# A state-space scan beside three convolution layers: a third PSUM bank for the scan's decays, made two ahead, and sums over states taken later

## The chip, the cores and the metric

The kernel runs on one core of one Trainium2 chip. The metric is the device time of one execution in microseconds (us). The median of three runs is 22843.68 us (22834.28 to 22850.13). A core has five engines that concern us, each with an instruction queue of its own: PE (TensorE, matrix multiplication), DVE (VectorE), ACT (ScalarE), POOL (GpSimd), and SP (SyncE), which here only issues DMAs. They meet through semaphores.

## What is computed

Four images of 128 channels and 128 x 128 pixels go through four layers. Each layer normalises its input by groups of channels and adds its result to it.

```python
x = x + _L0_conv_ref(_gn(x), ...)   # deformable 3x3 convolution (gathers rows by index)
x = x + _L1_conv_ref(_gn(x), ...)   # dilated 5x7 convolution and two 1x1
x = x + _L2_conv_ref(_gn(x), ...)   # state-space scan in four directions
x = x + _L3_conv_ref(_gn(x), ...)   # 3x3 convolution and a difference term
```

The core of layer 2, for each of four directions over the 16384 pixels, each channel and each of 16 states:

```python
dA = jnp.exp(d[..., None] * A)
h = h * dA + (d * u)[..., None] * b[:, :, None, :]
y = jnp.einsum('bkcn,bkn->bkc', h, c)
```

`dA` is what the kernel calls a decay. All data are fp32.

## The kernel before

The image is cut into 32 blocks of 4 rows, so a tile is 128 partitions x 512 pixels (2 KB per partition, one PSUM bank). The kernel uses all eight PSUM banks: two for `pa` (the decays), one for `dub`, one for `yacc`, and four "side banks", `bank(0)` to `bank(3)`, that the other layers share.

**The scan** (`scan`, from L761) is the long work. It runs over `seq`, 4 directions x 32 blocks, 128 blocks `t` for an image. The 128 channels x 16 states of a block are packed as four groups `g` of 32 channels; in each group a partition holds one channel and one of four sets of states, and four scans `ng` follow each other. One scan is a *slot*: 16 slots for each block, 2048 for each image, 8192 in all. In a group:

- DVE multiplies inputs and b for all four slots into `h` (L923, 128 x 2048); the inputs come from PSUM tile `dub`, which ACT fills (`inputs_up`, L838) in the slot `ng == 2` of the group before.
- For each slot ACT makes a decay (`decay`, L852, an exponential into `pa`), and DVE runs the scan (L963), which reads `pa` and replaces `h` in place. The decay of the next slot is issued just before the scan of this one. A `pa` tile can be written again when the scan two slots earlier has read it.
- After two scans ACT copies the last column into `carry` (`carry_on`, L887), and then POOL multiplies the two halves of `h` by c (`outputs`, L893): the first half at `ng == 2` of the same group, the second at the start of the next group. Beside layer 0 DVE takes the second half, at `ng == 2`. Where PE is the busier neighbour POOL also adds the two parts of each second half in every other group (L895), so that PE has one matmul less.
- PE sums over the states by a gathering matrix into `yacc` (`sums`, L866), and in the two backward directions adds the y of the forward pass (L871). Before the change group g's first half is summed at `ng == 2` of the next group and its second half at `ng == 3`.
- At the second group of block t (`g == 1`, `ng == 1`) `finish` has ACT copy the `yacc` of block t-1 out (L876) and stores it; `yacc` is one bank, so the next block's first sum waits for that copy.
- `prepare` (L791 to L823) makes steps, b and c of the block two ahead, in pieces, one after each slot.

**The other layers** run beside the scan: beside the scan of image b come layers 2 (after the scan) and 3 of image b-1, and layers 0, 1 and 2 (before the scan) of image b+1. They are generators; `together` lets the scan issue a slot and then pulls side work until it has reached the same share of its own length. `chain` and the weights in `head` and `tail` give these shares. Inside a layer, `weave` works through a hand-written order of groups: an entry `(n, step)` does step for the block n rounds back. `keep_order` then fixes the program order on every engine as issued. So each engine runs its queue in exactly the order in which the Python code emitted it, side work and scan mixed.

`loads` (L1221) sets `beside["busy"]` while a layer is the neighbour: "POOL" for layer 0, "PE" for layer 1, layer 2 before the scan, and the tail layers for the first images. This is how the scan knows what runs beside it.

The side banks in layer 2: before the scan, `pd2` (L637) and `pz` (L722) use bank 2 and `pv2` (L648) bank 3; after it `pd3` uses bank 0, `pv3` (L1045) bank 1, `pj3` bank 2 and `pv4` (L1071) bank 3. In both parts ACT reads a `pv` by Ln and Exp (`rsqrt`, L203 and L204), and `square` reads `pd2` twice (L643, L645). Layer 0 uses all four side banks; its table, layer 1 and layer 3 use banks 0 to 2 or fewer.

```python
for ng in range(NG):
    ...
    nc.vector.tensor_tensor_scan(o, f, o, carry[:, n : n + 1], ALU.mult, ALU.add)
    if ng == 3 and then[0] < len(seq):
        decay(*then, 0)
    next(more, None)
    yield (t * NST + n + 1) / slots
```

Of the kernel before, what the change touches and what calls it, by code (L numbers as in the profile page):

```python
# [10 lines left out]
F32 = mybir.dt.float32  # L11
# [7 lines left out]
P = 128  # L19
# [4 lines left out]
N = R * W  # L24
NBLK = H // R
KK = 9
NST = 16
# [4 lines left out]
NG = 4  # L32
# [78 lines left out]
def conv_preact_kernel(ctx: ExitStack, tc: tile.TileContext, a: dict, nb: int):  # L111
# [9 lines left out]
    pss = ctx.enter_context(tc.tile_pool(name="scps", bufs=1, space=PSUM))  # L121
# [7 lines left out]
    def bank(which, name):  # L129
        return psb.tile([P, N], F32, name=name, tag=f"bank{which}")  # L130

    waiting = []
    beside = {}

    def store(dst, src, after=3, of=None):

        waiting.append([after, of, dst, src])
# [459 lines left out]
    def layer2_pre(st):  # L597
# [6 lines left out]
        with ExitStack() as s:  # L604
# [26 lines left out]
            got = {}  # L631
# [13 lines left out]
                nc.scalar.activation(sq, pd, AF.Square, bias=shc)  # L645

            def spread_variance(i):
                got["v", i] = pv = bank(3, "pv2")  # L648
                nc.tensor.matmul(pv, jmat, got["s", i], start=True, stop=True)

            def invert(i):
# [109 lines left out]
    def scan(st, pull):  # L761
        us = st["u"]
        st["y"] = ys = (image("yrow"), image("ycol"))
        seq = []
# [3 lines left out]
            seq += [(k, i, back, back) for i in order]  # L768
        carries = {}
        blocks = [{} for _ in seq] + [None]  # L770

        def fetch(t):
            if t < len(seq):
                k, i, _, _ = seq[t]
                while st["out"] < (i + 1 if k == 0 else NBLK + 1):
                    pull()
                    tick()
                if not stored(us[0]):
                    flush()
                blocks[t]["u"] = load(sp, blk(us[k % 2], i), [P, N], "u", bufs=2)  # L780
# [64 lines left out]
                p.rearrange("p n t -> p (n t)"), src.unsqueeze(0).to_broadcast([Q, P // Q, NG * N])  # L845
            )

        def decay(t, g, ng):
            k = seq[t][0]
            n = g * NG + ng  # L850
            pa = pss.tile([P, N], F32, name="pa", bufs=2)
            nc.scalar.activation(pa, blocks[t]["p", g][:, 0, :], AF.Exp, scale=neg_a[:, k, n : n + 1])  # L852
            blocks[t]["a", n] = pa

        def sums(t, g, half):

            c = blocks[t]
            k, i, back, second = seq[t]
            if g == 0 and half == 0:
                c["y"] = pss.tile([P, N], F32, name="yacc")  # L860
            last = g == NG - 1 and half == 1
            parts = (2 * half, 2 * half + 1)
            if half and c.get(("added", g)):
                parts = parts[:1]
            for ng in parts:
                nc.tensor.matmul(  # L866
                    c["y"], gather[:, g, :], c["h", g][:, ng, :],
                    start=g == 0 and ng == 0, stop=last and ng == parts[-1] and not second,
                )
            if last and second:  # L870
                nc.tensor.matmul(c["y"], ident, c["before"], start=False, stop=True)  # L871

        def finish(t):
            k, i, back, second = seq[t]
            y = sp.tile([P, N], F32, name="y")
            nc.scalar.copy(y, blocks[t]["y"])  # L876
            store(blk(ys[k % 2], i), y, of=ys)
            blocks[t] = None
            st["summed"] = t + 1 - 3 * NBLK
# [9 lines left out]
        def outputs(t, g, half, engine=nc.gpsimd):  # L889

            c = blocks[t]
            h = c["h", g][:, 2 * half : 2 * half + 2, :]
            engine.tensor_mul(h, h, c["cb"][:, 2 * half : 2 * half + 2, :])  # L893
            if half and g % 2 and beside.get("busy") == "PE":
                engine.tensor_add(h[:, 0, :], h[:, 0, :], h[:, 1, :])  # L895
                c["added", g] = True
# [10 lines left out]
        for g in range(2):  # L907
            spread_steps(0, g)
        inputs_up(0, 0)
        decay(0, 0, 0)  # L910
        slots = len(seq) * NST
        for t, (k, i, back, second) in enumerate(seq):
            c = blocks[t]
            carry = carries[k]
            more = prepare(t + 2) if t + 2 < len(seq) else iter(())
            if t > 0:
                fetch(t + 3)
            for g in range(NG):
                then = (t, g + 1) if g + 1 < NG else (t + 1, 0)
                soon = (t, g + 2) if g + 2 < NG else (t + 1, g + 2 - NG)  # L920
                before = (t, g - 1) if g else (t - 1, NG - 1)
                c["h", g] = h = hp.tile([P, NG, N], F32, name="h")
                nc.vector.tensor_tensor(  # L923
                    h, c["pdu", g].unsqueeze(1).to_broadcast([P, NG, N]), c["bb"], ALU.mult
                )
                on_vector = beside.get("busy") == "POOL"
                if before[0] >= 0:
                    carry_on(*before, 1)
                    if not on_vector:
                        outputs(*before, 1)  # L930
                if soon[0] < len(seq):
                    spread_steps(*soon)
                decay(t, g, 1)
                if g == 1:
                    if t + 1 < len(seq):
                        spread_states(t + 1, "bb")
                if g == 2 and t + 1 < len(seq):
                    spread_states(t + 1, "cb")
                if g == 3 and second:
                    c["before"] = load(sp, blk(ys[k % 2], i), [P, N], "before")  # L940
                for ng in range(NG):
                    n = g * NG + ng
                    if ng == 1:
                        decay(t, g, 2)
                        if g == 1 and t > 0:
                            finish(t - 1)
                    if ng == 2 and before[0] >= 0 and on_vector:
                        outputs(*before, 1, nc.vector)
                    if ng == 2:
                        carry_on(t, g, 0)  # L950
                        outputs(t, g, 0)
                        decay(t, g, 3)
                        if then[0] < len(seq):
                            inputs_up(*then)
                        if before[0] >= 0:
                            sums(*before, 0)
                    if ng == 3:
                        if before[0] >= 0:
                            sums(*before, 1)
                    o, f = h[:, ng, :], c["a", n]  # L960
                    if back:
                        o, f = o[:, ::-1], f[:, ::-1]
                    nc.vector.tensor_tensor_scan(o, f, o, carry[:, n : n + 1], ALU.mult, ALU.add)  # L963
                    if ng == 3 and then[0] < len(seq):
                        decay(*then, 0)
                    next(more, None)
                    yield (t * NST + n + 1) / slots
            for _ in more:
                pass
        t = len(seq) - 1  # L970
        carry_on(t, NG - 1, 1)
        outputs(t, NG - 1, 1)
        sums(t, 3, 0)
        sums(t, 3, 1)
        finish(t)
# [3 lines left out]
    def layer2_post(st):  # L979
# [4 lines left out]
        with ExitStack() as s:  # L984
# [18 lines left out]
            got = {}  # L1003
# [64 lines left out]
                nc.scalar.activation(sq, p, AF.Square)  # L1068

            def spread_out(i):  # L1070
                got["w", i] = pv = bank(3, "pv4")  # L1071
                nc.tensor.matmul(pv, jmat, got["t", i], start=True, stop=True)

            def invert_out(i):
# [21 lines left out]
            def r(what):  # L1096
                return lambda n: what(NBLK - 1 - n)

            def ready(n):
                return st["summed"] > min(n, NBLK - 1) and stored(st["y"])  # L1100

            order = [[(0, r(fetch)), (1, r(fetch_gate)), (5, r(fetch_skip))], [(2, r(centre))],
                     [(3, r(spread_variance))], [(7, r(affine))], [(5, r(spread_out))], [(2, r(square))],
                     [(3, r(invert))], [(7, r(add))], [(5, r(invert_out))], [(4, r(project))],
                     [(3, r(gated))], [(6, r(scale))], [(7, r(measure))], [], [(4, r(square_out))], []]
            yield from weave(NBLK, order, ready)
            flush()
        st["x3"], st["stats3"] = keep, stats_out
# [109 lines left out]
    sts = [{"b": b} for b in range(nb)]  # L1218
    last = nb - 1

    def loads(engine, stage):  # L1221
        for f in stage:
            beside["busy"] = engine
            yield f
        beside.clear()

    def head(b):
        st = sts[b]
        return [(layer0_table(st), 12), (loads("POOL", layer0(st)), 28), (loads("PE", layer1(st)), 14),
                (loads("PE", layer2_pre(st)), 36)]  # L1230

    def tail(b):
        load = "PE" if b + 1 < last else None
        return [(loads(load, layer2_post(sts[b])), 16), (loads(load, layer3(sts[b])), 22)]

    first = head(0)
    drain(chain(first[:3]))
# [1 line left out]
    for b in range(nb):  # L1239
        side = [(begun, 18)] if b == 0 else tail(b - 1)  # L1240
        if b < last:
            side += head(b + 1)
        else:
            side = [(stage, 2.5 * w) for stage, w in side] + [(layer2_post(sts[b]), 33)]
        together(lambda pull: scan(sts[b], pull), chain(side))
    drain(layer3(sts[last]))
    keep_order(tc, started)
# [83 lines left out]
```

## Time and profile before

| what | us |
|---|---|
| median of 3 runs | 22843.68 |
| the profiled execution, its own time | 22841.14 |
| its span (first to last instruction) | 22839.3 |
| the first scan starts at | 2120.1 |
| the last scan starts at | 22509.2 |
| beside layer 0, in three stretches | 6100 |
| DVE scans, 8192 x 1270 ns | 10076.9 |
| DVE products into h, 2048 x 2268 ns | 4645.6 |
| ACT decays, 8192 x 686 ns | 5618.4 |
| POOL products with c, 3740 x 2360 ns | 8783.5 |
| PE sums, 15354 instructions | 8369.2 |

The busy tenths by slice, 40 slices of 571 us, show the stages: the scan begins at the end of the fourth, and the three stretches where DVE is at 9 and ACT at 8 are those beside layer 0.

```profile
PE   4558866667788887666788888666688878777778
DVE  3553889999988799889997789889998788999883
ACT  5885768887677666788768666688867866666563
POOL 4772777777887887787787798778878778877773
PEclk7669988888899998888899999888899989899899
```

In a row of the groups, the figures after the bar are the busy time, the mean length of one instruction in ns, and then the time that the engine stood idle just before these instructions, with the releaser that ended most of it. In the waits, each row names the waiting engine and line, what it waited for, the total, how often, and the longest. In a table by stretch the columns are the stretch, its length, then busy time and number of instructions of PE, PE's weight loads (PEld), DVE, ACT and POOL, the granted PE clock, the DMA share and GB/s. A line of the timeline has start, length, engine, line and operation, and in brackets the idle time before it and its releaser.

### The profile page before, as it was taken

Reading aid. Unit: us, or ns where it says so; the run is one execution under the profiler, and the core shown is the slowest. Engines: PE = TensorE matmul, PEld = TensorE weight load, DVE = VectorE, ACT = ScalarE, POOL = GpSimd, SP = SyncE. Lnnn points to the kernel's source line nnn. Section 1 sums busy time; section 2 is a strip of 40 time slices with the busy share of each in tenths; the row PEclk is TensorE's granted clock in tenths of the full one; section 3 lists DMA queues with packets and bytes.
Section 4 is the critical chain, followed back from the end, with each engine's and each line's share of the span. In section 5 each row is a group of like instructions: output and inputs, shape, how many; then the busy total and the mean of one; then the engine's idle time right before and its main releaser. Section 6 shows DMA issues by size and latency. Waiting matters only on the chain. (4 is left out here: it accounts for less than half of the span.)

```text
span 22839.3 us, 178643 instructions
## 1 busy us (share of the span) xinstructions
PE 17184.5 (75%) x38114; PEld 6655.5 (29%) x38114; DVE 18850.6 (83%) x19637; ACT 16473.3 (72%) x37410; POOL 17338.8 (76%) x11579
## 2 busy tenths in 40 slices
PE   4558866667788887666788888666688878777778
PEld 1222222223232333222333233222232323233323
DVE  3553889999988799889997789889998788999883
ACT  5885768887677666788768666688867866666563
POOL 4772777777887887787787798778878778877773
PEclk7669988888899998888899999888899989899899
DMA  8775587777665957777766775877775677555664
GB/s 241 231 219 156 193 285 241 241 240 242 217 203 188 231 199 265 241 243 244 245 215 201 200 219 205 281 241 243 245 245 196 201 203 216 185 192 200 195 200 120
DMA packets 2557775, 5005.30 MB, mean 219 GB/s; under 512 B 1056832, under 2 KB 1328648, under 8 KB 2414352
## 3 DMA queue, kind: packets, MB, share of 16 engines
q1 hardware_dynamic: 2188048, 3785.60, 50.7%
q0 software_dynamic: 368640, 1208.25, 17.9%
q8 instruction: 310, 5.08, 0.1%
q14 instruction: 777, 6.37, 0.1%
HBM read 4065.12 MB, written 857.74 MB: 216 GB/s over the span
## 5 line engine op out<-in xcount | busy, mean ns | idle before, releaser
L963 DVE TENSOR_TENSOR_SCAN h<-pa,carry,h 128x512 f32<-128x512 f32 x8192 | 10076.9, 1270 | 1516.3 <-ACT pa L852 1307.6
L893 POOL TENSOR_TENSOR h<-h,cb 128x1024 f32<-128x1024 f32 x3740 | 8783.5, 2360 | 2996.6 <-ACT carry L887 2925.3
L866 PE MATMUL yacc<-h,gather_sb 128*128 128x512 f32 x15354 | 8369.2, 678 | 1722.1 <-POOL h L893 851.3
L852 ACT ACTIVATE pa<-spread,neg_a 128x512 f32<-128x512 f32 x8192 | 5618.4, 686 | 3412.6 <-DVE h L963 3385.3
L416 POOL DMA_INDIRECT g<-table,idx x4608 | 4552.8, 988 | 1603.3 <-issue 1075.9
L923 DVE TENSOR_TENSOR h<-dub,bb 128x2048 f32<-128x2048 f32 x2048 | 4645.6, 2268 | 434.2 <-ACT dub L838 427.8
L866 PEld LDWEIGHTS yacc<-h,gather_sb 128*128 128x128 f32 x15354 | 3135.0, 216 | 6166.8 <-issue 3593.4
L430 ACT ACTIVATE g<-g,wt 128x128 f32<-128x128 f32 x9216 | 2895.2, 390 | 398.5 <-DMA g<-table,idx 394.3
L453 PE MATMUL pst<-ident,v 128*128 128x128 f32 x4608 | 1178.7, 364 | 2141.3 <-DVE v L445 1885.1
L442 DVE TENSOR_TENSOR pw<-pw,g 128x512 f32<-128x512 f32 x2304 | 1599.0, 694 | 956.9 <-ACT pw L430 900.0
L430 ACT ACTIVATE pw<-g,wt 128x128 f32<-128x128 f32 x4608 | 1693.1, 367 | 262.1 <-DVE v L445 149.3
L453 PEld LDWEIGHTS pst<-ident,v 128*128 128x128 f32 x4608 | 716.3, 158 | 3535.7 <-issue 1890.8
L463 PE MATMUL acc<-smp,w_sb 128*128 128x512 f32 x2304 | 1573.8, 773 | 15.2 <-DVE x L470 12.5
L445 DVE SCALAR_TENSOR_TENSOR v<-g,wt,pw 128x128 f32<-128x128 f32 x4608 | 1293.7, 343 | 113.4 <-DVE pw L442 2.3
L838 ACT COPY dub<-spread 128x512 f32<-128x512 f32 x2048 | 1169.1, 571 | 138.3 <-DMA spread<-stepsd 138.0
L887 ACT COPY carry<-h 128x2 f32<-128x2 f32 x4096 | 766.7, 187 | 694.2 <-DVE h L963 692.6
L807 PE MATMUL pxbc<-u,xbc_sb 128*128 128x512 f32 x1024 | 664.2, 735 | 737.9 <-DVE h L923 725.3
L791 PE MATMUL pdt<-u,wd 128*128 128x512 f32 x1024 | 626.8, 697 | 684.1 <-DVE h L923 609.6
L1164 PE MATMUL p<-xn,w_l_sb 128*128 128x508 f32 (+2 forms) x2304 | 1105.0, 599 | 1.8 <-ACT xn L1143 1.8
L703 PE MATMUL px<-win,convw_sb 128*128 128x508 f32 (+1 forms) x1536 | 851.9, 637 | 6.7 <-DMA win<-win 6.7
L705 PE MATMUL py<-win,diag 128*64 128x508 f32 (+1 forms) x1536 | 833.7, 625 | 0.0
L817 POOL TENSOR_TENSOR e<-e,one_e 128x512 f32<-128x512 f32 x512 | 668.5, 1306 | 87.1 <-ACT one_e L811 87.1
(170 smaller groups left out, 17301.6 us busy)
## 6 DMA issues: line engine op xcount, KB each, us to landing
spread<-stepsd SPq DMA_DIRECT2D x2048, 512.0 KB, 4.2
bb<-bcd SPq DMA_DIRECT2D x512, 1024.0 KB, 7.5
cb<-bcd SPq DMA_DIRECT2D x512, 1024.0 KB, 7.7
stepsd<-steps SPq DMA_DIRECT2D x512, 512.0 KB, 3.0
table<-gt SPq DMA_DIRECT2D x512, 256.0 KB, 5.9
g<-table,idx POOLq DMA_INDIRECT x4608, 3.8
u<-urow SPq DMA_DIRECT2D x256, 256.0 KB, 4.5
yrow<-y SPq DMA_DIRECT2D x256, 256.0 KB, 3.1
```

The source lines that it names most:

```text
L416: nc.gpsimd.indirect_dma_start(out=g[:, r].rearrange("p q c -> p (q c)"), out_offset=None, in_=table, in_offset=bass.IndirectOffsetOnAxis( ...
L430: nc.scalar.activation(pw[:, r * P : (r + 1) * P] if c == 0 else g[:, r, c, :], g[:, r, c, :], AF.Copy, scale=wv[:, r, q, k, c : c + 1],)
L442: nc.vector.tensor_add(pw, pw, g[:, :, c, :])
L445: nc.vector.scalar_tensor_tensor(v[:, r, :], g[:, r, 3, :], wv[:, r, q, k, 3:4], pw[:, r, :], ALU.mult, ALU.add)
L453: nc.tensor.transpose(pst[:, r * P : (r + 1) * P], v[:, r, :], ident)
L463: nc.tensor.matmul(got["a", i], w0[:, k, :], got.pop(("c", n)), start=k == 0, stop=k == KK - 1)
L838: nc.scalar.copy(p, blocks[t]["p", g][:, 1, :])
L852: nc.scalar.activation(pa, blocks[t]["p", g][:, 0, :], AF.Exp, scale=neg_a[:, k, n : n + 1])
L866: nc.tensor.matmul(c["y"], gather[:, g, :], c["h", g][:, ng, :], start=g == 0 and ng == 0, stop=last and ng == parts[-1] and not second,)
L893: engine.tensor_mul(h, h, c["cb"][:, 2 * half : 2 * half + 2, :])
L923: nc.vector.tensor_tensor(h, c["pdu", g].unsqueeze(1).to_broadcast([P, NG, N]), c["bb"], ALU.mult)
L963: nc.vector.tensor_tensor_scan(o, f, o, carry[:, n : n + 1], ALU.mult, ALU.add)
```

## The change

Four things change.

1. `loads` takes a flag `spare`, true for every neighbour but layer 0. With it, `decays` issues decays up to two slots ahead of the scan instead of one, and every third decay goes to side bank 3 as `pa3`.
2. To free bank 3, `pv2` moves to bank 2 and `pv4` to bank 1, and the hand-written order after the scan is changed around them.
3. `sums`: a group's first half is issued at `ng == 3` of the next group, its second half at `ng == 1` of the group after that.
4. `finish` is issued at `ng == 2` instead of `ng == 1`.

```diff
             def spread_variance(i):
-                got["v", i] = pv = bank(3, "pv2")
+                got["v", i] = pv = bank(2, "pv2")
...
+        ahead = {"turn": -1, "made": 0}
+        def decays(at):
+            while ahead["made"] < min(at + (2 if beside.get("spare") else 1) + 1, len(seq) * NST):
+                decay(ahead["made"])
+                ahead["made"] += 1
...
-        def decay(t, g, ng):
+        def decay(n):
+            t, n = divmod(n, NST)
+            g, ng = divmod(n, NG)
             k = seq[t][0]
-            n = g * NG + ng
-            pa = pss.tile([P, N], F32, name="pa", bufs=2)
+            turn = (ahead["turn"] + 1) % 3
+            if turn == 2 and not beside.get("spare"):
+                turn = 0
+            ahead["turn"] = turn
+            pa = bank(3, "pa3") if turn == 2 else pss.tile([P, N], F32, name="pa", bufs=2)
             nc.scalar.activation(pa, blocks[t]["p", g][:, 0, :], AF.Exp, scale=neg_a[:, k, n : n + 1])
...
+                earlier = (t, g - 2) if g > 1 else (t - 1, g + NG - 2)
...
-                decay(t, g, 1)
+                at = t * NST + g * NG
+                decays(at)
...
                     if ng == 1:
-                        decay(t, g, 2)
-                        if g == 1 and t > 0:
-                            finish(t - 1)
+                        decays(at + 1)
+                        if earlier[0] >= 0:
+                            sums(*earlier, 1)
+                    if ng == 2 and g == 1 and t > 0:
+                        finish(t - 1)
...
                         carry_on(t, g, 0)
                         outputs(t, g, 0)
-                        decay(t, g, 3)
+                        decays(at + 2)
                         if then[0] < len(seq):
                             inputs_up(*then)
-                        if before[0] >= 0:
-                            sums(*before, 0)
-                    if ng == 3:
-                        if before[0] >= 0:
-                            sums(*before, 1)
+                    if ng == 3 and before[0] >= 0:
+                        sums(*before, 0)
...
-                    if ng == 3 and then[0] < len(seq):
-                        decay(*then, 0)
+                    if ng == 3:
+                        decays(at + 3)
...
             def spread_out(i):
-                got["w", i] = pv = bank(3, "pv4")
+                got["w", i] = pv = bank(1, "pv4")
...
-                     [(3, r(spread_variance))], [(7, r(affine))], [(5, r(spread_out))], [(2, r(square))],
-                     [(3, r(invert))], [(7, r(add))], [(5, r(invert_out))], [(4, r(project))],
-                     [(3, r(gated))], [(6, r(scale))], [(7, r(measure))], [], [(4, r(square_out))], []]
+                     [(3, r(spread_variance))], [(7, r(affine))], [(2, r(square))], [(3, r(invert))], [],
+                     [(5, r(spread_out))], [(7, r(add))], [(4, r(project))], [(5, r(invert_out))],
+                     [(3, r(gated))], [(6, r(scale))], [(7, r(measure))], [(4, r(square_out))], []]
...
-    def loads(engine, stage):
+    def loads(engine, stage, spare=False):
         for f in stage:
-            beside["busy"] = engine
+            beside["busy"], beside["spare"] = engine, spare
             yield f
         beside.clear()
```

In `head`, `tail` and the last image, the layers other than layer 0 are wrapped in `loads(..., True)`.

More of the change, by code (lines that the diff above doesn't have):

```diff
@@ L909, in scan @@
         inputs_up(0, 0)
-        decay(0, 0, 0)
+        decays(-1)
         slots = len(seq) * NST
@@ L972, in scan @@
         outputs(t, NG - 1, 1)
+        sums(t, 2, 1)
         sums(t, 3, 0)
@@ L1228, in head @@
         st = sts[b]
-        return [(layer0_table(st), 12), (loads("POOL", layer0(st)), 28), (loads("PE", layer1(st)), 14),
-                (loads("PE", layer2_pre(st)), 36)]
+        return [(loads(None, layer0_table(st), True), 12), (loads("POOL", layer0(st)), 28), (loads("PE", layer1(st), True), 14),
+                (loads("PE", layer2_pre(st), True), 36)]
     def tail(b):
         load = "PE" if b + 1 < last else None
-        return [(loads(load, layer2_post(sts[b])), 16), (loads(load, layer3(sts[b])), 22)]
+        return [(loads(load, layer2_post(sts[b]), True), 16), (loads(load, layer3(sts[b]), True), 22)]
     first = head(0)
@@ L1243, in conv_preact_kernel @@
         else:
-            side = [(stage, 2.5 * w) for stage, w in side] + [(layer2_post(sts[b]), 33)]
+            side = [(stage, 2.5 * w) for stage, w in side] + [(loads(None, layer2_post(sts[b]), True), 33)]
         together(lambda pull: scan(sts[b], pull), chain(side))
```

## The prediction

> **What bounds the kernel now.** I read four views in this order: the busy times of the page, its groups by line, the waits, and the busy times by stretch; then the timeline at one stall.
>
> ```profile
> PE 17184.5 (75%) x38114; PEld 6655.5 (29%) x38114; DVE 18850.6 (83%) x19637; ACT 16473.3 (72%) x37410; POOL 17338.8 (76%) x11579
> L963 DVE TENSOR_TENSOR_SCAN h<-pa,carry,h 128x512 f32<-128x512 f32 x8192 | 10076.9, 1270 | 1516.3 <-ACT pa L852 1307.6
> L852 ACT ACTIVATE pa<-spread,neg_a 128x512 f32<-128x512 f32 x8192 | 5618.4, 686 | 3412.6 <-DVE h L963 3385.3
> L876 ACT COPY y<-yacc 128x512 f32<-128x512 f32 x512 | 295.8, 578 | 30.8 <-PE yacc L871 30.8
> ```
>
> No engine is full, VectorE is nearest, and the two middle rows are the matter: VectorE waits 1307.6 us for decays in 1076 stalls, while ScalarE waits 3385.3 us for scans before making decays. Each starves the other. The waits view says where else engines stand:
>
> ```profile
> DVE h L963 <- ACT pa L852: 1307.6, 1076, 7.4
> PEld yacc L866 <- POOL h L893: 1619.8, 1006, 7.4
> PE yacc L866 <- POOL h L893: 851.3, 521, 6.6
> PE yacc L866 <- ACT y L876: 398.0, 270, 6.5
> DVE pw L442 <- ACT pw L430: 900.0, 524, 10.7
> ```
>
> By stretch (PE, PEld, DVE, ACT, POOL) the limits differ. In order: layer 0, layer 2 before the scan, layer 2 after it, and layer 3, each beside a scan.
>
> ```profile
> 9190.00:11180.00 1990.00, 1286.15 (x3309) 525.08 (x3302) 1790.33 (x2718) 1717.84 (x4756) 1566.72 (x1375) 0.82 0.75 241
> 17200.00:18380.00 1180.00, 1031.30 (x2102) 354.58 (x2102) 951.20 (x673) 916.97 (x1684) 916.25 (x502) 0.95 0.59 195
> 7400.00:8010.00 610.00, 497.89 (x982) 186.27 (x981) 435.75 (x325) 420.95 (x817) 525.96 (x322) 0.92 0.88 222
> 19750.00:21360.00 1610.00, 1257.02 (x2714) 510.18 (x2714) 1537.53 (x1114) 975.21 (x1971) 1271.37 (x646) 0.95 0.54 195
> ```
>
> Beside layer 3 VectorE is 96% busy, in the second line it is 81% with PE at 87%, and in the third POOL leads with 86%. One stall of the second kind, ScalarE and then VectorE:
>
> ```profile
> 17499.75 1.28 ACT L735 ACT_TABLE_LOAD   x1
> 17501.04 1.06 ACT L735 ACTIVATE u<-u 128x1024 f32<-128x1024 f32 x1
> 17502.00 1.04 ACT L736 ACTIVATE z<-z 128x1024 f32<-128x1024 f32 x1
> 17503.06 1.28 ACT L737 ACT_TABLE_LOAD   x1
> 17504.35 0.69 ACT L852 ACTIVATE pa<-spread,neg_a 128x512 f32<-128x512 f32 x1
> ...
> 17505.08 1.28 DVE L963 TENSOR_TENSOR_SCAN h<-pa,carry,h 128x512 f32<-128x512 f32 x1 [4.23 <-ACT pa L852]
> 17509.07 1.28 DVE L963 TENSOR_TENSOR_SCAN h<-pa,carry,h 128x512 f32<-128x512 f32 x1 [2.71 <-ACT pa L852]
> ```
>
> A burst of side work stands between two decays in ScalarE's queue. VectorE had one decay in store, used it, and stood 4.23 us, then 2.71 us in the same burst.
>
> **What the Trainium skill says.** "Perfetto Trace Analysis", Optimization Strategy: the same gap repeating on the engine that should be saturated can mean that PSUM or SBUF ran out for the next tile. The trace fits: 1076 such gaps, with two buffers for pa. The same page, Tensor Engine Instruction, says that ScalarE, VectorE and GpSimd take instructions strictly in order; in the lines above the decay of 17504.35 does follow the side work. "PSUM — Partial Sum Buffer", Specifications: eight banks of 512 fp32 values. A 128x512 tile fills one, and the kernel uses all eight, so the third pa can only come from a side bank; no run here shows the count itself. "Perfetto Trace Analysis", Identifying the Most-Contended Engine, warns that matmul busy time misstates PE's distance from its limit. So I don't read PE's 87% as a hard ceiling; PEld is 30% in the same stretch.
>
> **The change part by part.** *Third bank, decays two ahead (outside layer 0).* No instruction is added: 8192 decays of 686 ns before and after. Decay n+2 is issued where decay n+1 was, and its bank was last read by scan n-1, the same scan that decay n+1 waited for. So ScalarE's wait for VectorE is no longer than before, and nothing queued behind it is later because of it. What changes is VectorE's store: two decays at the start of a burst. dub (571 ns), the other thing VectorE needs from ScalarE, is already issued two slots ahead.
>
> To price it I went through the timeline by stage. I took the stalls between two points at which ScalarE waited over 0.1 us for a scan (there it has caught up) as one group, and let each group give back at most one scan, 1.27 us. Stalls and what they can return: layer 2 before the scan (four stretches) 717 us, return 277; layer 2 after it (four) 348, return 162; layer 3 (three) 98, return 94; layer 0's table (three) 54, return 52; layer 1 (three) 56, return 53. Sum of returns 638. The rest, 35 us, lies in layer 0 and the tail, where no third bank is used or little is left. A store that covers a group's first operation too (four scans and one 2.27 us product per four slots, 1.84 us per slot) would return about 780.
>
> How much arrives? In layer 3, the table and layer 1 VectorE is 87% to 96% busy and the stalls are short; I take 0.9 of 199, 179 us. In the two parts of layer 2 other engines are close: taking 74 us out of 1180 raises PE from 87% to 93%, and 26 out of 610 raises POOL from 86% to 90%. I take 0.65 of 439, 285 us, a choice between a third and all.
>
> *Sums two slots (second half) and one slot (first half) later.* The same matmuls. Each now follows its POOL product by five slots, instead of four (first half) or three (second), so most of PE's 851 us wait on POOL goes. I book nothing for it: ScalarE hardly waits for PE, so PE was not holding the loop. It gives PE the room that the line above assumes. The h tile is held two slots longer; with four buffers the next write of the same one is still seven slots behind the last read (nine before), so no wait.
>
> *finish one slot later.* Its copy (578 ns) now follows the last sums by one slot, not two. In the trace those sums ended a median of 2.4 to 4.6 us before the copy beside all but layer 0, where it was 7.5; a slot is about 2.1 us there and 4.4 in layer 0. So some of the 512 copies will wait. Behind it on ScalarE stand carry, the decay and dub. Bounds: nothing, if PE runs as far ahead as its lost POOL waits allow, and 512 x 1 us if not; I take 25 us. The y store goes to SP a slot later; its nearest reader, the load of before at the turn of direction, still comes some three slots after it.
>
> *Side banks.* pv2 joins pd2 and pz in bank 2; pv4 joins pv3 in bank 1 and the order after the scan changes. The matmul of pv2 must now wait until square has read pd2 (3 groups of the weave earlier), and pv4 until Ln has read pv3 (2 groups earlier). About 256 such hand-overs, 128 of each. ScalarE reaches its next read 3 groups later; a group is about 0.6 slot in the first weave (576 slots for 38 rounds of 25 groups) and 0.4 or more in the second (256 for 39 rounds of 16), so 2.6 us or more cover a 1.0 us matmul. I cost it at nothing; uncovered, it is in the rival below. Layer 0 (6100 us of the scan) keeps its two banks and its order of decays: no gain, no loss.
>
> Sum: 179 + 285 - 25 = 439. From the profiled execution, 22841.1 us (span 22839.3 and 1.8 around it), this gives 22402; the median 22843.7 is 2.5 above that execution. Forecast 22400.
>
> **The rivals.** (1) *Only the VectorE-bound stages gain.* For it: PE at 87% to 89% before the scan, POOL at 86% after it. Against: all VectorE idle time of the second stretch is this wait (196 of 229 us). Then 179 - 25 = 154 come, 22690. (2) *The wait moves and nothing is gained:* ScalarE's bursts are as long as before, and VectorE stands later instead. For it: in the example one scan covers 1.27 of 6.94 us. Against: ScalarE still waits 162 us for scans in that stretch, so it does catch up and refills. 22840. (3) *Slower: the merged banks put PE and ScalarE on one chain.* In layer 2, PE waits for square's two reads (0.68 us each) and then ScalarE for pv2 (1.0), 2.4 us a block; after the scan Ln (0.69) and pv4 (1.0), 1.7 us. If all reach VectorE: 128 x 2.4 + 128 x 1.7 = 525 us lost against 439 gained, 22930. It decides from 439 / 256 = 1.7 us per hand-over on. For it: PE waits 398 us for y, so it does run level with ScalarE. Against: the three groups between the steps, and a stage in which PE's POOL waits end. (4) *The third bank is not used where I think:* the compiled order of the changed kernel shows every third decay in its own tile before and after the scan, so I give this nothing.
>
> **How the numbers follow.** Forecast 0.63, its own range 22150 to 22640; rival 1 0.13; rival 2 0.07; rival 3 0.17. From 22050 (the 780 us bound gives 22060) to 22850 the range leaves out rival 3 and little else. A difference under 0.2% (46 us) can't be told from none. Faster 0.76, same 0.07, slower 0.17.
>
> **What would show it.** Right: the row of the scan waits under 800 us for pa in place of 1307.6; the stretch beside layer 3 near 98% VectorE; PE's waits for h from POOL cut by half or more; y's wait for yacc under 100 us. Wrong: the pa stalls stay above 1100 us, or the waits of sq and pv (L203, L649, L1072) grow from tens to hundreds, which is rival 3, or a new line of y behind yacc of some hundreds.

## The result and the profile after

The changed kernel takes 22660.5 us (22655.8 to 22664.7, four runs) against 22845.3 us (22834.3 to 22850.1) for the kernel before on the same chip: a ratio of 0.9924, 95% interval 0.9911 to 0.9936. That is 0.76% faster, some 175 us; the two medians themselves lie 185 us apart. The sign of the forecast was right; 439 us had been expected, so more than half of the gain is missing.

The groups of the page of the changed kernel that answer to those above, the row of VectorE's product, which had not been shown (before: 4645.6 us busy, 434.2 us idle ahead of it), and that of PE's sums:

```profile
L977 DVE TENSOR_TENSOR_SCAN h<-pa,carry,h 128x512 f32<-128x512 f32 x8192 | 9982.2, 1267 | 366.8 <-ACT pa L865 273.2
L865 ACT ACTIVATE pa<-spread,neg_a 128x512 f32<-128x512 f32 x8192 | 5623.7, 687 | 3143.9 <-DVE h L977 3048.8
L937 DVE TENSOR_TENSOR h<-dub,bb 128x2048 f32<-128x2048 f32 x2048 | 4659.6, 2275 | 1356.9 <-ACT dub L845 763.4
L879 PE MATMUL yacc<-h,gather_sb 128*128 128x512 f32 x15354 | 8241.4, 666 | 1073.3 <-POOL h L906 626.4
```

The wait at the scan is nearly gone: idle time ahead of scans fell from 1516.3 to 366.8 us. But idle time ahead of the products rose from 434.2 to 1356.9 us. Of 1150 us removed in one place, 923 came back one instruction later in VectorE's own queue. The waits of the changed kernel name the parties:

```
DVE h L937 <- issue: 539.7, 294, 6.9
ACT y L889 <- PE yacc L884: 232.1, 150, 7.6
ACT y L889 <- PE yacc L879: 99.0, 102, 4.2
```

These three are new in their size: the product waits 540 us with no releaser named (5 us before), and the copy of `finish` waits 331 us for PE's sums (31 us before). PE's wait for POOL fell by a quarter only, from 851.3 to 626.4 us. We then counted the waits of over 0.15 us ahead of the 2048 products by their group in the block: 448 us ahead of the first group's (405 before), 231 ahead of the second's (28 before), 583 ahead of the third's (below 1 before), 91 ahead of the fourth's. The third group's is the one just behind `finish`.

By stretch, the same four stages, cut where the same scans start and end as in the four stretches before:

```
9108.60:11114.60 2006.00, 1292.31 (x3312) 532.98 (x3304) 1801.42 (x2718) 1718.92 (x4756) 1566.35 (x1375) 0.80 0.75 239
17084.30:18231.50 1147.20, 1025.10 (x2104) 356.14 (x2102) 951.15 (x674) 912.08 (x1684) 915.98 (x502) 0.95 0.62 200
7332.10:7951.30 619.20, 503.41 (x982) 189.09 (x982) 435.88 (x326) 421.10 (x817) 524.88 (x321) 0.91 0.87 218
19569.80:21187.10 1617.30, 1293.41 (x2714) 530.89 (x2714) 1533.30 (x1114) 977.98 (x1971) 1270.33 (x646) 0.91 0.55 194
```

Before the scan of layer 2 the stretch is 3% shorter (1180 to 1147 us). Beside layer 0 and after the scan nothing was gained (16 and 9 us longer). In the longest stretch beside layer 3, where VectorE had 96% and the surest gain was booked, the length has not fallen either (1610 to 1617 us), and VectorE has 95%. One of its stalls in the timeline of the changed kernel (idle time and releaser in brackets):

```
19667.57 2.27 DVE L937 TENSOR_TENSOR h<-dub,bb 128x2048 f32<-128x2048 f32 x1
19669.87 4.81 DVE L977 TENSOR_TENSOR_SCAN h<-pa,carry,h 128x512 f32<-128x512 f32 x4
19669.89 1.13 PE L814 MATMUL pxbc<-u,xbc_sb 128*128 128x512 f32 x2 [2.47 <-DVE h L937]
...
19670.85 3.24 PE L879 MATMUL yacc<-h,gather_sb 128*128 128x512 f32 x4
...
19674.13 0.58 ACT L889 COPY y<-yacc 128x512 f32<-128x512 f32 x1 [1.14 <-PE yacc L879]
...
19674.71 0.69 ACT L865 ACTIVATE pa<-spread,neg_a 128x512 f32<-128x512 f32 x1
...
19675.33 0.58 ACT L845 COPY dub<-spread 128x512 f32<-128x512 f32 x1
...
19676.00 2.29 DVE L937 TENSOR_TENSOR h<-dub,bb 128x2048 f32<-128x2048 f32 x1 [1.32 <-issue]
```

This reads from top to bottom as one chain. VectorE's product of the second group ends at 19669.84 and frees the one bank of `dub`; PE's `pxbc` matmul, which takes that bank, had waited 2.47 us for it. Behind `pxbc` in PE's queue stand the block's last sums, now at slot 5 instead of slot 3. They end at 19674.09; the copy of `finish` waits for them, and `carry`, decay and `dub` wait behind the copy. `dub` is ready at 19675.9. VectorE had finished its four scans at 19674.68 and stood for 1.32 us, with a decay in store that it could not use before the product. So here the row "issue" is a wait for `dub` in all but name. Of the 294 waits of this kind 248 stand ahead of a third group's product, about one in every second block.

The copy waits in 252 of its 512 turns. In 123 of these (144 of the 331 us) PE had just been held at `pxbc` by VectorE's product, as here; in 90 others (125 us) PE's last hold was at `pdt`, the first matmul of `prepare`, which takes the same bank and so waits for the first group's product. From the end of the last sums to the start of the copy the median over all blocks is now 0.04 us; it was 4.0 us.

### The profile page after: what moved, and what is told of

It is laid out like the page before. It is cut to its first block, busy times and chain, and to the rows that moved or that the text cites. A ratio compares the mean times of both kernels' runs of the same rounds, so it can differ in the third digit from the quotient of the medians.

```text
span 22660.2 us, 176842 instructions
## 1 busy us (share of the span) xinstructions
PE 17088.4 (75%) x38114; PEld 6670.4 (29%) x38114; DVE 18822.5 (83%) x19637; ACT 16470.1 (73%) x37410; POOL 17330.0 (76%) x11579
## 5 line engine op out<-in xcount | busy, mean ns | idle before, releaser
L977 DVE TENSOR_TENSOR_SCAN h<-pa,carry,h 128x512 f32<-128x512 f32 x8192 | 9982.2, 1267 | 366.8 <-ACT pa L865 273.2
L879 PE MATMUL yacc<-h,gather_sb 128*128 128x512 f32 x15354 | 8241.4, 666 | 1073.3 <-POOL h L906 626.4
L937 DVE TENSOR_TENSOR h<-dub,bb 128x2048 f32<-128x2048 f32 x2048 | 4659.6, 2275 | 1356.9 <-ACT dub L845 763.4
L798 PE MATMUL pdt<-u,wd 128*128 128x512 f32 x1024 | 769.3, 842 | 1133.2 <-DVE h L937 1016.3
```

Of the source, the lines that this page charges most:

```text
L879: nc.tensor.matmul(c["y"], gather[:, g, :], c["h", g][:, ng, :], start=g == 0 and ng == 0, stop=last and ng == parts[-1] and not second,)
L937: nc.vector.tensor_tensor(h, c["pdu", g].unsqueeze(1).to_broadcast([P, NG, N]), c["bb"], ALU.mult)
```

## The experiments

Three theories. **F**: the late `finish` costs, as in this chain. **D**: `dub` has a single bank, so decays ahead only move the wait there. **B**: the merged side banks cost. The kernels ran in three groups, each on one chip with the kernel before beside it. The kernel before took 23293, 22819 and 23313 us in the three, so only ratios are compared. Where an expectation names a time in us, the ratio times 22845 is set against it.

### First group: the parts

**`finish` after `dub`**, the changed kernel with one move:

```diff
-                    if ng == 2 and g == 1 and t > 0:
-                        finish(t - 1)
...
                         decays(at + 2)
                         if then[0] < len(seq):
                             inputs_up(*then)
+                        if g == 1 and t > 0:
+                            finish(t - 1)
```

> The changed kernel, with the copy of finish issued after carry, decay and dub of its slot instead of ahead of them. Theory F (the copy waits for the last sums and holds dub, and so the product of the third group): the 583 us of waits ahead of the third group's products fall below 150, and the time to about 22300 us (22150 to 22450). Theory D (dub has one bank, so two decays ahead only move VectorE's wait to the product, whatever stands in the queue): 22600 to 22670 us, the waits for dub stay. Theory B (the merged side banks hold PE and ScalarE): about 22660 us, no change.

Measured: 0.9821 (0.9805 to 0.9837). The groups of this kernel's page:

```profile
L977 DVE TENSOR_TENSOR_SCAN h<-pa,carry,h 128x512 f32<-128x512 f32 x8192 | 9985.8, 1267 | 424.8 <-ACT pa L865 321.9
L937 DVE TENSOR_TENSOR h<-dub,bb 128x2048 f32<-128x2048 f32 x2048 | 4654.9, 2273 | 1068.0 <-ACT dub L845 766.7
L879 PE MATMUL yacc<-h,gather_sb 128*128 128x512 f32 x15354 | 8155.8, 661 | 980.2 <-ACT y L889 515.4
```

In the waits, the copy's own wait falls from 331 to 98 us, and the waits ahead of the third group's products from 583 to 182 us (F had said under 150). PE now waits for the copy (the third row's releaser), 515 us, at no visible price. Idle time ahead of scans and products together, the first two rows, is 424.8 + 1068.0 = 1493 us against 1724 in the changed kernel: 231 us less, and 1.0% of the time is what the ratio fell by (0.9924 to 0.9821, in two groups). The ratio answers to 22436 us, at the slow end of F's range. F holds; D and B, which expected no move, fall as the main cause.

The longest stretch beside layer 3 shows it most plainly. VectorE's largest wait there, in the kernel before, the changed one and this one:

```
DVE h L963 <- ACT pa L852: 49.3, 95, 1.5
DVE h L937 <- issue: 71.8, 50, 3.4
DVE h L937 <- issue: 2.3, 4, 0.7
```

The change took away 49 us of waits for decays and put 72 us ahead of the product in their place; behind `dub` the copy leaves 2 us. From its first to its last instruction this layer took 1615, 1618 and 1543 us in the three kernels, and VectorE has 99% in the last. PE's granted clock there was 0.95, 0.91 and 0.92, so the lower clock is not what held the changed kernel.

**Bank only**: third bank, decays two ahead, merged side banks; sums and `finish` as before.

```diff
                     if ng == 1:
                         decays(at + 1)
-                        if earlier[0] >= 0:
-                            sums(*earlier, 1)
-                    if ng == 2 and g == 1 and t > 0:
-                        finish(t - 1)
+                        if g == 1 and t > 0:
+                            finish(t - 1)
...
                             inputs_up(*then)
+                        if before[0] >= 0:
+                            sums(*before, 0)
                     if ng == 3 and before[0] >= 0:
-                        sums(*before, 0)
+                        sums(*before, 1)
...
-        sums(t, 2, 1)
         sums(t, 3, 0)
```

> The changed kernel's third bank, two decays ahead and merged side banks, with the sums and finish in their places of before. Theory F: without the late finish the bank alone gives about 22400 us (22250 to 22550), less than the changed kernel takes. Theory D: about 22660 us, the waits sit at dub as in the changed kernel. Theory B: about 22660 us or more.

Measured: 0.9878 (0.9861 to 0.9894). It is better than the whole change: the change to sums and `finish` takes away part of what the bank gives. But at 22566 us it lies just outside F's range (22250 to 22550). Two groups of its page go with this:

```profile
L879 PE MATMUL yacc<-h,gather_sb 128*128 128x512 f32 x15354 | 8314.5, 674 | 1722.4 <-POOL h L906 862.6
L937 DVE TENSOR_TENSOR h<-dub,bb 128x2048 f32<-128x2048 f32 x2048 | 4660.2, 2275 | 1150.4 <-ACT dub L845 826.2
```

PE is held by POOL as before (863 us), ScalarE waits 243 us for `pdt` (the row of e behind pdt in the waits; 152 before), ahead of `dub`, and the product waits 826 us for `dub` (428 before). We read this as one chain; no run takes it apart. So a part of D is true: what is left of the wait sits at `dub`. With the late sums and the copy behind `dub` the ratio goes from 0.9878 to 0.9821. The bank with the early sums and the copy behind `dub` was not run, so how much of this belongs to the sums and how much to the place of the copy is open.

**Sums only**: the changed kernel with `spare` never set, so that decays are one ahead in two banks everywhere.

```diff
-            beside["busy"], beside["spare"] = engine, spare
+            beside["busy"], beside["spare"] = engine, False
```

> The changed kernel without the third bank: decays one ahead in two banks everywhere, the sums and finish late, side banks merged. Theory F: the late finish now meets a store of one decay, so slower than the kernel before by 150 to 400 us, about 23100. Theory D: sums and finish do nothing, about 22845 us. Theory B: 22900 to 23100 us as well, but with the added waits at the reads of pv and pd and not at y.

Measured: 1.0133 (1.0116 to 1.0150), slower, as F said. VectorE's wait is back at the scan, and larger than the 1307.6 us of before:

```profile
L977 DVE TENSOR_TENSOR_SCAN h<-pa,carry,h 128x512 f32<-128x512 f32 x8192 | 10074.3, 1269 | 1751.3 <-ACT pa L865 1534.9
```

In the waits, y stands 296 us behind PE's sums, about as in the changed kernel (331), and the second spread waits 106 us for Ln, about as in the changed kernel too (97). With a store of one decay the stalls of ScalarE reach VectorE as waits for `pa`.

**Banks and order only**: the kernel before with `pv2` in bank 2, `pv4` in bank 1 and the new order after the scan.

> The kernel before, with the two side banks merged and the new order after the scan, nothing else. Theories F and D: within 50 us of 22845. Theory B: slower by 100 to 300 us, with the waits of sq and pv (Ln, the second spread) in the hundreds.

Measured: 1.0039 (1.0024 to 1.0053), about 90 us. This missed F and D (within 50 us) and falls just short of B (100 to 300 us, with waits in the hundreds). From here the parts can be set side by side in one group: bank against this kernel 0.9878 / 1.0039 = 0.984, or 1.6% gained; sums and `finish` without the bank 1.0133 / 1.0039 = 1.009, or 0.9% lost. The parts don't simply add: beside the late sums and the late `finish` the bank takes the ratio from 1.0133 to 0.9924, which is 2.1%, so the deeper store also covers part of what they cost.

### Second group: where the merged banks cost

> The changed kernel once more, on the chip of the three runs beside it, so that the parts can be set against the whole. Theory F, theory B and theory D alike: ratio 0.990 to 0.994 to the kernel before.

The unaltered changed kernel: 0.9923 (0.9907 to 0.9940), as at first.

Before the scan, `pv2` alone in bank 2:

```diff
-                got["v", i] = pv = bank(3, "pv2")
+                got["v", i] = pv = bank(2, "pv2")
```

> The kernel before with pv2 moved from bank 3 to bank 2 and nothing else. If the 0.39% of the merged banks lies before the scan (hand-over of pd2 to pv2): ratio 1.003 to 1.004. If it lies after the scan: 1.000 within its interval.

Measured: 1.0006 (0.9997 to 1.0015), not told from nothing. After the scan, `pv4` in bank 1 and the new order:

> The kernel before with pv4 moved from bank 3 to bank 1 and the new order after the scan, pv2 left in bank 3. If the cost lies after the scan: ratio 1.003 to 1.004, with the waits of the second spread for Ln (67 us with both merged, 5 before). If before it: 1.000.

Measured: 1.0029 (1.0017 to 1.0040). In its waits the second spread stands 67.7 us behind Ln (53 times; no such row before), and Ln 37.4 us behind the second spread (14.2 before). The four stretches after the scan are together 64 us longer than before, about what the ratio says. At the end of it stands the scan, from 1307.6 to 1366.2 us:

```profile
L963 DVE TENSOR_TENSOR_SCAN h<-pa,carry,h 128x512 f32<-128x512 f32 x8192 | 10074.4, 1269 | 1574.9 <-ACT pa L852 1366.2
```

Then both ways to avoid that hand-over: the changed kernel with `finish` after `dub` and `pv4` in bank 2 beside `pj`,

```diff
-                got["w", i] = pv = bank(1, "pv4")
+                got["w", i] = pv = bank(2, "pv4")
...
-                     [(3, r(spread_variance))], [(7, r(affine))], [(2, r(square))], [(3, r(invert))], [],
-                     [(5, r(spread_out))], [(7, r(add))], [(4, r(project))], [(5, r(invert_out))],
-                     [(3, r(gated))], [(6, r(scale))], [(7, r(measure))], [(4, r(square_out))], []]
+                     [(3, r(spread_variance))], [(7, r(affine))], [(5, r(spread_out))], [(2, r(square))],
+                     [(3, r(invert))], [(7, r(add))], [(5, r(invert_out))], [],
+                     [(3, r(gated))], [(4, r(project))], [(6, r(scale))], [(7, r(measure))], [], [(4, r(square_out))]]
```

> The changed kernel with finish after dub, and with pv4 in bank 2 beside pj, in nearly the order of before (spread of the projection ahead of square, project two groups later), so that pv4 waits for no Ln of pv3. If the merged bank 1 costs what theory B still claims: 0.978 to 0.980, some 60 us under the 0.9821 of the kernel with finish after dub. If it doesn't: 0.982.

Measured: 0.9808 (0.9791 to 0.9824). Its neighbour in the same group is the changed kernel at 0.9923, so the two repairs are worth 1.15%, here within one group. Whether the second adds anything to the first (0.9821, in another group) is inside the intervals.

### Third group: what about `finish` it is

**Last sums early**: `finish` stays ahead of `dub`, but the last sums of a block go back to slot 3, ahead of `pxbc`.

```diff
-                        if earlier[0] >= 0:
+                        if earlier[0] >= 0 and earlier[1] < NG - 1:
                             sums(*earlier, 1)
...
                     if ng == 3 and before[0] >= 0:
                         sums(*before, 0)
+                        if g == 0:
+                            sums(*before, 1)
```

> The changed kernel, only that a block's very last sums (second half of its fourth group) are taken at slot 3 of the next block, ahead of the matmul for b and c, as before the change; finish stays ahead of dub at slot 6. If finish costs because its copy waits for those sums, which stand behind a matmul that waits for VectorE: y's waits for yacc (331 us in the changed kernel) fall under 80 us and the ratio to 0.982 to 0.985. If the copy itself ahead of dub is what costs (0.58 us in each block): 0.989 to 0.992, near the changed kernel's 0.9923.

Measured: 0.9882 (0.9865 to 0.9898), between both expectations. The copy no longer waits (28 us), as the first one said; but the time does not follow all the way. The product's group in this kernel's page:

```profile
L937 DVE TENSOR_TENSOR h<-dub,bb 128x2048 f32<-128x2048 f32 x2048 | 4660.4, 2276 | 1249.1 <-ACT dub L845 777.6
```

The idle time is 108 us less than the changed kernel's 1356.9, where `finish` after `dub` has 289 less. Now `pxbc` stands behind the last sums, and the copy `bc`, which stands at slot 5 ahead of `dub`, waits 207 us for it (58 in the changed kernel). The waits ahead of the third group's products are still 439 us. So taking away the copy's wait gives back 0.4% of the 1.0%. In its place `bc`, which also stands ahead of `dub`, now waits for PE. That this makes up the rest is likely but not shown; the copy's own 0.58 us and `bc` were not taken apart further.

**`finish` at slot 7**, ahead of the next block's first sum:

```diff
-                    if ng == 2 and g == 1 and t > 0:
+                    if ng == 3 and g == 1 and t > 0:
                         finish(t - 1)
```

(with the line moved below `inputs_up`).

> The changed kernel with finish at slot 7, just ahead of the next block's first sum, two slots after the last sums instead of one, and behind dub of slot 6. Theory F: as finish after dub or a little better, 0.979 to 0.983. If PE suffers because its next sum now follows the copy at once: 0.985 to 0.990.

Measured: 0.9810 (0.9793 to 0.9826), as `finish` after `dub`. PE's wait for the copy grows to 710 us, again at no visible price.

**Order only after the scan**, all banks as before:

> The kernel before with the new order after the scan, all banks as they were. If the 0.29% of that part is the hand-over in bank 1 (pv4 waits until Ln has read pv3): 1.000 within 0.0015. If it is the order itself: 1.002 to 1.004.

Measured: 1.0005 (0.9996 to 1.0014). The order alone is not told from nothing, so the 0.29% is the hand-over in bank 1.

**Both repairs**, `finish` at slot 7 and `pv4` beside `pj`:

> Both repairs together, finish at slot 7 and pv4 in bank 2 beside pj: 0.977 to 0.981, the best of all if finish at slot 7 is at least as good as finish after dub (0.9808 with the same banks).

Measured: 0.9811 (0.9794 to 0.9827), in one group with 0.9810 without the second repair. So the second repair shows no gain here; the hand-over, which costs 0.29% in the kernel before, seems to be covered by decays two ahead, though the intervals leave room for some 0.2%. `finish` after `dub` or at slot 7 is thus the whole repair: 1.8% to 1.9% under the kernel before, against 0.76% for the change as it is.

## Why the prediction was off, step by step

*The step that failed is the term for `finish`: 25 us were taken, about 230 us were paid (give or take 50).* The text gave its bounds as nothing and 512 x 1 us and chose the low end, "if PE runs as far ahead as its lost POOL waits allow". The distance between last sums and copy was read from the trace as a time (median 2.4 to 4.6 us) and one slot was taken off. What was not asked is what the sums were moved past: between slot 3 and slot 5 of PE's queue stands `pxbc` at slot 4, which waits for VectorE's product (725 us ahead of `pxbc` in the page of before). So PE is not free to run ahead there, whatever POOL does. The chain product, `pxbc`, sums, copy, `dub`, product then closes in one group's time, as in the stall above. PE's wait for POOL, most of which was to go, fell by a quarter only. That the place of `finish` ahead of `dub` has this price is shown by experiment: 0.9923 to 0.9821 over two groups (0.9808 within one, with the second repair), 231 us in idle time. That `pxbc` makes the sums late is shown in the trace for half of the copy's waits; taking the sums ahead of it gave 0.4% back, and made `bc` wait for `pxbc` instead.

*The third bank: 464 us were taken, about 1.6%, 365 us, measured.* That is the bank beside the early sums, give or take 50 us; beside the late ones it is 2.1%. The mechanism was right: the scan's wait for `pa` is 273 us (under 800 was named), ScalarE's wait for scans did not grow (3385 to 3049). Taken alone its size is a fifth lower, and `dub`, which was dismissed as "already issued two slots ahead", is the likely reason. It is issued so, but with decays also two ahead it is the next thing VectorE lacks: in the bank-only kernel the product waits 826 us for it, 398 more than before.

*The late sums: nothing booked, 0.57% gained together with the copy behind `dub`* (0.9878 to 0.9821; the two were not parted). "ScalarE hardly waits for PE" was not quite so before (152 us at e for `pdt`) and less so with the bank alone (243 us). PE's wait for POOL did not halve in the changed kernel (851 to 626 us); with `finish` out of the way it does (371 us).

*The side banks: nothing booked, 0.39% lost alone.* Before the scan the cover held (0.06%, within noise). After it, the 2.6 us cover did not hold each time: the second spread waited for Ln at 53 of 128 hand-overs. The 0.29% is about 0.5 us for each of the 128, well below the 1.7 us from which this rival would have decided; with the third bank and `finish` repaired it is not seen.

*By stage.* The forecast's terms beside what the traces show, in us gained. A stage is counted from the first to the last instruction of its layer, in the stretches beside a scan (the first one before the scan of layer 2 only in its later part). The last column is the kernel with both `finish` after `dub` and `pv4` beside `pj`. A second trace of the changed kernel agrees within 11 us in each row.

| stage | forecast | changed | repaired |
|---|---|---|---|
| layer 2 before the scan | 180 | 136 | 172 |
| layer 2 after the scan | 105 | 8 | 47 |
| layer 3 | 85 | 32 | 134 |
| layer 0's table and layer 1 | 95 | 12 | 77 |
| layer 0 | 0 | -18 | 11 |

The 25 us for `finish` were not given to a stage. In the changed kernel three rows lost most of what was booked. Layer 0, with 6100 us, neither gained nor lost more than 0.3% in all, as said.

*The signs.* Of the four named for being right one came, the scan's wait under 800 us. VectorE beside layer 3 stayed at 95% instead of 98%, PE's waits for POOL fell by a quarter instead of half, and y's wait for yacc is 331 us instead of under 100. That last row is also a sign named for being wrong, "a new line of y behind yacc of some hundreds". Of the rivals the second, that the wait moves, came nearest in kind: 923 of 1150 us moved, but to the product, which it had not named.

The repaired kernel stands at 0.981 to 0.982, where 22400 us is 0.981. That the sum fits it is in part luck: by stage it was too high after the scan and too low beside layer 3, and by part the smaller bank and the larger sums cancel.

Still open is the rest at `dub`: 231 us of waits ahead of the second group's products in the changed kernel, 268 in the one with `finish` after `dub`. A second bank for it was not tried; no bank is free.

## What to carry to other kernels

When a buffer is made deeper, list everything that the consumer needs from the same producer queue and look at the next item: the wait can move there, and then anything put ahead of it in that queue that waits for a third engine can set the pace. When a step is moved later in an in-order queue, ask what it is moved past, not only by how much; one matmul that waits for the consumer can close the loop. A copy that only frees a buffer is best put behind the instructions that feed the critical engine, as long as whoever waits for the freed buffer has time to spare; here PE waited 515 to 710 us for it without a loss.

## What was not expected of the hardware

VectorE's scans took less of its time when they followed each other: in the timelines 1.28 us for one alone, but 4.81 us for four in a row, 1.20 each. One record still lasts 1.26 us on average in such a row; the records overlap at their ends. Four in a row came 563 times before and 1274 times in the changed kernel. The busy time of the 8192 scans fell from 10076.9 to 9982.2 us, 95 us which the sum had not booked; with decays one ahead again (sums only) it is 10074.3.

The same kernel before took 22819 us on one chip and 23313 on another, 2.2% apart, while the changed kernel's ratio came out as 0.9924 and 0.9923 in two groups. Most of the difference lies in one place that the change doesn't touch: layer 0 of the first image, which runs before any scan, took 1476 to 1480 us in all traces of the second group, and 1895 to 1918 us in those of the first and third. Why is not shown.
